# First attention: transposes by 64 rows into two banks, one PSUM rotation of four two-bank tiles, two projections to a tile

## The chip, the core and the metric

One core of a Trainium2 chip runs the whole program in one launch. The time is device microseconds from one execution. Before the change it is 716.13 us, the median of three runs (715.78 to 716.39).

The engines are TensorE (PE, with its weight loads shown apart as PEld), VectorE (DVE), ScalarE (ACT), GpSimd (POOL) and SyncE (SP, which issues most DMAs). PSUM, the memory TensorE writes its products to, has eight banks of 512 fp32 values per partition.

## The reference, cut to what matters

Two layers, each x = x + attention(norm(x)) * silu(ffn(norm(x))), for four batches of 512 tokens of width 128. The change touches only the attention of the first layer, which walks through each batch in 8 segments of 64 tokens and carries a memory M and its sum Z along (16 heads of 64):

```
q, k, v = x @ Wq, x @ Wk, x @ Wv            # per batch (8, 64, 16*64)
for each segment:                            # lax.scan
    scores  = q k^T / 8, causal
    att_dot = softmax(scores) v
    sq, sk  = elu(q) + 1, elu(k) + 1
    att_mem = sq M / (sq Z^T)
    M, Z    = M + sk^T v, Z + sum(sk)
    out     = (gate * att_mem + (1 - gate) * att_dot) @ Wo
```

The first layer's gate (its FFN), the second layer's mixture of experts and its attention over 16 channels are left as they were, but for the PSUM tiles that a few steps of the second FFN take while the first attention still runs.

## The kernel before, in words

`run` (L2310) goes through the norm and FFN of layer one, then `attn0` (L568), then `ffn1` and `attn1` of the second layer. Nearly every instruction goes through `pin` (L332), by way of `mm1`, `act1` and `vec1` (L335 to L342), which keeps it at its place in program order on its engine. So lines 336 and 339 stand for most matmuls and ScalarE steps in the profile, and the tiles tell them apart. The order of the work around the change is the order in which the code below writes it; each engine takes its own instructions in that order, and waits where a tile that it needs is not yet written or not yet free.

`attn0` has 32 segments, numbered n (8 per batch). One segment n, in program order (L833 to L877):

- `elu_exp(n+1, 0)`: ScalarE, exp and relu of q (tiles elu, up);
- `scores(n+1)`: TensorE, 16 matmuls into tile sc; VectorE evicts it (E);
- `memory(n)`: TensorE into mm; VectorE takes the reciprocal and evicts it, GpSimd applies the gate (L736);
- `elu(n+1, 0)`: VectorE (L684);
- `attended(n-2)`: four transposes of 128 rows by 128 columns into tile pa (L785); ScalarE evicts it by four instructions into attT;
- `keys(n+1)`: four such transposes into tile pk (L691); ScalarE evicts it into sk;
- `update(n)`: TensorE into mu, VectorE adds it to the memory mz (L751);
- `attend(n)`: TensorE into dot; VectorE divides, GpSimd gates and adds (L774, L775);
- `elu_exp(n+2, 1)` on ScalarE;
- up to four projection chunks of a later half batch (L601 to L642), with `scores_exp(n+1)` (ScalarE, E) behind the first of them. A chunk fills one bank: pp for q and k, with 8 matmuls that the profile shows as 16, [...]evicted by ScalarE into pj; or pv for v, evicted into vt by ScalarE (by VectorE for the first two halves), from where SP sends it to DRAM (vd) and back as vone;
- every fourth segment has no chunks but `output`: 32 matmuls (64 shown) into po.

Twelve chunks belong to each half batch: four v chunks in segments with n % 4 = 3, then four of k, then four of q. The first half's twelve chunks and two of the second's stand ahead of the loop. Steps of the second FFN (sums, normed, turned, hidden, logits, chosen, placed, up) are put in between segments 18 to 30 by a table in `run` (L2341 to L2350).

PSUM has two rotations, in one pool that stays open through `ffn1`. Tag "w" has three tiles of two banks: sc, mm, mu, dot, po (L596). Tag "t" has two tiles of one bank: pa, pk and the projection chunks (L599). The second FFN's steps use the same two tags (L924, L1006, L1038, L1072, L1081). A tile of a rotation is written again only when its last reader is done.

Of the kernel before, what the change touches and what calls it, by code (L numbers as in the profile page):

```python
# [12 lines left out]
F32 = mybir.dt.float32  # L13
# [3 lines left out]
AF = mybir.ActivationFunctionType  # L17
# [91 lines left out]
class Kernel:  # L109
# [234 lines left out]
    def pool1(self, ins):  # L344
        return self.pin(ins)

    def dma1(self, out, in_):
        return self.pin(self.nc.sync.dma_start(out=out, in_=in_))

# [215 lines left out]

    def attn0(self, xnT, g0, stack, psum, between):  # L568

# [16 lines left out]
        for k in range(4):  # L588
            t = pool.tile([P, 4, 2, DK + 1], F32, name=f"vone{k}", bufs=1)
            nc.gpsimd.memset(t[:, :, :, DK : DK + 1], 1.0)  # L590
            vone.append(t)
        qkv, vd, attT, seg = {}, {}, {}, {}

        def wide(name):

            return psum.tile([P, 2, S], F32, name=name, tag="w", bufs=3)  # L596

        def narrow(name):
            return psum.tile([P, S], F32, name=name, tag="t", bufs=2)  # L599

        def project(h):  # L601


            if h >= 2 * B:
                return []
            qkv[h] = dst = [
                pool.tile([P, 32, 64], F32, name=f"pj{h}_{wi}", tag=f"pj{wi}")
                for wi in range(2)
            ]
            vd[h] = drams.tile([2, P * 16, DK], F32, name=f"vd{h}", tag="vd")  # L610
            def chunk_v(p, k):
                ps = narrow(f"pv{h}_{p}_{k}")
                self.mm1(
                    ps, lhsT=xnT[h // 2][:, h % 2 * 2 + p, :],
                    rhs=self.wqkv[2][:, k * S : (k + 1) * S], start=True, stop=True,
                )
                t = pool.tile([P, S], F32, name=f"vt{h}_{p}_{k}", tag="vt")
                if h > 1:
                    self.act1(t, ps, AF.Copy)
                else:  # L620
                    self.vec1(nc.vector.tensor_copy(t, ps))
                nc.sync.dma_start(
                    out=vd[h][p].rearrange("(q k c) d -> k q (c d)", k=2, c=8)[k], in_=t
                )

            def chunk(wi, cq):
                ps = narrow(f"pp{h}_{wi}_{cq}").rearrange("p (c k) -> p c k", c=4)
                for c4 in range(4):
                    c = cq * 4 + c4
                    for p in range(2):  # L630
                        self.mm1(
                            ps[halves[p], c4, :],
                            lhsT=self.wqkv[wi][:, c * 64 : c * 64 + 64],
                            rhs=xnT[h // 2][:, h % 2 * 2 + p, :], start=True, stop=True,
                        )
                view = dst[wi].rearrange("d k (t c) -> d (k t) c", c=16)
                self.act1(
                    view[:, :, cq * 4 : cq * 4 + 4], ps.rearrange("d c k -> d k c"), AF.Copy
                )
            qk = [(lambda wi=wi, cq=cq: chunk(wi, cq)) for wi in (1, 0) for cq in range(4)]  # L640
            v = [(lambda p=p, k=k: chunk_v(p, k)) for p in range(2) for k in range(2)]
            return v + qk if h else qk[:4] + v + qk[4:]  # L642
# [41 lines left out]
            self.vec1(nc.vector.scalar_tensor_tensor(t, t, 1.0, up, ALU.min, ALU.add))  # L684
            seg[n][w] = t

        def turn(n, src, name):

            ps = narrow(f"{name}{n}").rearrange("p (hp c) -> p hp c", hp=4)
            for hp in range(4):  # L690
                self.pin(nc.tensor.transpose(  # L691
                    ps[:, hp], src[:, 2 * hp : 2 * hp + 2, :].rearrange("d a j -> d (a j)"),
                    self.ident,
                ))
            return ps.rearrange("p hp (x d) -> p hp x d", x=2)

        def keys(n):
            t = pool.tile([P, 4, 2, DK], F32, name=f"sk{n}", tag="sk")
            self.act1(t, turn(n, seg[n][1], "pk"), AF.Copy)
            seg[n]["sk"] = t  # L700

        def values(n):

# [71 lines left out]
            nc.gpsimd.tensor_add(t, t, seg[n]["t1"])  # L775
            seg[n]["att"] = t

        def attended(n):

            if n % 4 == 0:  # L780

                attT[n // 4] = pool.tile([P, 16, 4, 32], F32, name=f"attT{n}", tag="attT")
            ps = narrow(f"pa{n}").rearrange("p (hp c) -> p hp c", hp=4)
            for hp in range(4):
                self.pin(nc.tensor.transpose(  # L785
                    ps[:, hp, :], seg[n]["att"][:, hp].rearrange("i p v -> i (p v)"),
                    self.ident,
                ))
            src = ps.rearrange("p (a u) (h t c) -> p c a u h t", a=2, h=2, c=16)
            dst = attT[n // 4][:, :, n % 4].rearrange("p c (u y t) -> p c u y t", u=2, y=4)  # L790
            for h in range(2):
                for a in range(2):
                    self.act1(dst[:, :, :, (a + h) % 2 * 2 + a], src[:, :, a, :, h], AF.Copy)
# [20 lines left out]
        for i, chunk in enumerate(todo):  # L814
            chunk()
            if i == 4:
                elu_exp(0, 1)
            if i == 7:
                elu(0, 1)
            if i == 9:  # L820
                keys(0)
        ahead = project(1)
        for n in range(2):
            values(n)
# [8 lines left out]
        for n in range(nseg):  # L833
            if n % 4 == 3:
                todo = project((n + 1) // 4 + 1)
            elif n == 0:
                todo = ahead
            each = 2 if n == 0 else 4 if n < 3 or n % 4 != 2 else 0
            nxt = n + 1 < nseg
            more = nxt and not last(n + 1)  # L840
            if n + 2 < nseg:
                values(n + 2)
            if nxt:
                elu_exp(n + 1, 0)
                scores(n + 1)
            memory(n)
            if nxt:
                elu(n + 1, 0)
            if n > 1:
                attended(n - 2)  # L850
            if more:
                keys(n + 1)
            if not last(n):
                update(n)
            for f, *args in between.get(n - 0.5, []):
                f(*args)
            attend(n)
            ahead = n + 2 < nseg and not last(n + 2)
            if ahead:
                elu_exp(n + 2, 1)  # L860
            chunks, todo = todo[:each], todo[each:]
            for chunk in chunks[:1]:
                chunk()
            if nxt:
                scores_exp(n + 1)
            if ahead:
                elu(n + 2, 1)
            for chunk in chunks[1:]:
                chunk()
            for f, *args in between.get(n - 0.25, []):  # L870
                f(*args)
            if n % 4 == 2 and n > 4:
                output(n // 4 - 1)
            if not nxt:
                attended(n - 1)
            for f, *args in between.get(n, []):
                f(*args)  # L877
        return [lambda: attended(nseg - 1), lambda: output(2 * B - 1)]

    def begin_ffn1(self, pool, psum, layer, rooms=False):
# [37 lines left out]
        def name(what, *at):  # L920
            return "_".join(map(str, (what, layer) + at))

        def narrow(what, *at):
            return psum.tile([P, 4, P], F32, name=name(what, *at), tag="t", bufs=2)  # L924

        def sums(b):
            self.norm_sums(pool, mv, layer, range(b * 4, b * 4 + 4))
# [75 lines left out]
            self.vec1(v.tensor_add(gw[:, tiles(b), :], at[:, :, 0], at[:, :, 1]))  # L1003

        def up(b, e):
            ps = psum.tile([P, 2, S], F32, name=name("ph", b, e), tag="w", bufs=3)  # L1006
            for c in range(2):
                self.mm1(
                    ps[:, c], lhsT=self.w_in[:, e, c * P : (c + 1) * P], rhs=xnT[b],
# [24 lines left out]
        def placed(b):  # L1034


            at, idf, mask, _ = picked[b]
            ps = psum.tile([P, 4, NE], F32, name=name("pn", b), tag="t", bufs=2)  # L1038
            self.mm1(ps, lhsT=before, rhs=mask, start=True, stop=True)
            t = place[b] = pool.tile([P, 4, NE], F32, name=name("place", b), tag="place", bufs=2)  # L1040
            self.vec1(v.scalar_tensor_tensor(t, ps, 1.0, mask, ALU.add, ALU.mult))
# [23 lines left out]
        def send(b, k):  # L1065

            if k == 0:
# [1 line left out]
                    "p e (k s) -> p e k s", k=4  # L1069
                )  # L1070
                rows[b] = self.rooms.tile([NE * 4 * ROOM, D], F32, name=name("rows", b))
            ps = psum.tile([P, NE, ROOM], F32, name=name("px", b, k), tag="w", bufs=3)  # L1072
            for part in range(3):
                self.mm1(
                    ps, lhsT=parts[b][:, part, k], rhs=marks[b, k],
# [2 lines left out]
            self.act1(sent[b][:, :, k], ps, AF.Copy)  # L1078

        def up2(b, i):  # L1080
            ps = psum.tile([P, 2, 2, 4 * ROOM], F32, name=name("ph", b, i), tag="w", bufs=3)  # L1081
            for e in range(2):
                for c in range(2):
                    self.mm1(
# [1225 lines left out]
    def run(self):  # L2310
# [15 lines left out]
        with tc.tile_pool(name="wf1", bufs=1) as wf1, tc.tile_pool(name="f1", bufs=1) as f1:  # L2326
# [4 lines left out]
                xnT, g0 = self.norm_ffn0(0, lambda pool, psum: self.mixing1(pool, late, psum))  # L2331
                self.load_memory(w0)
            self.load_experts(wf1)
            with tc.tile_pool(name="ap", bufs=1, space=PSUM) as psum:
                third = ExitStack()
                self.rooms = ctx.enter_context(
                    tc.tile_pool(name="rooms", bufs=1, space=bass.MemoryType.DRAM)
                )
                first = self.begin_ffn1(f1, psum, 1, True)

                left = self.attn0(xnT, g0, stack, psum, {  # L2341
                    18: [(first.sums, 0)], 19: [(first.sums, 1)],
                    20: [(first.roots, 0, 2)], 20.5: [(first.scale, 0, 2, False), (first.normed, 0)],
                    21: [(first.turned, 0), (first.normed, 1)],
# [3 lines left out]
                    24: [(first.placed, 1)], 25: [(first.chosen, 0)],  # L2348
                    30.5: [(first.up, 0, 0)],
                })  # L2350
                second, prep = ExitStack(), []

                def begin():
# [125 lines left out]
```

## Time and profile before

| what | us |
|---|---|
| median of three runs | 716.13 |
| the profiled execution, in all | 716.71 |
| its span, from first to last instruction | 715.3 |
| busy in the span: PE | 676.8 (95%) |
| busy: DVE, ACT, POOL | 501.3, 491.1, 344.4 |
| first attention, from its first projection to the last segment | about 77 to 319 |
| projections ahead of the loop | 77 to 91.5 |
| segments 0 to 2 | 91.5 to 114 |
| segments 3 to 20 (no step of the second layer's TensorE work among them) | 114 to 241 |
| segments 21 to 26, with steps of the second FFN | 241 to 297.2 |
| segments 27 to 31, no projections left | from 297.2 |

A group line of the profile names line, engine, operation, tiles written and read, count and busy time; idle time before an instruction is put down to what ended it, the releaser. In the timeline neighbouring instructions of one group are merged: start, length from the first start to the last end, count. TensorE's instructions overlap one another, so a matmul that reads 0.27 us may be followed by the next 0.05 us later; cadence is taken from starts. The granted TensorE clock is 0.994 on average.

### The profile page before, as it was taken

To read this page: it belongs to the slowest core of one execution; us is meant where nothing else is said; L and a number is where in the kernel's file an instruction comes from. 1 tells how busy PE (TensorE), PEld (TensorE's weight loads), DVE (VectorE), ACT (ScalarE), POOL (GpSimd) and SP (SyncE) were. 2 spreads that over 40 slices of the span, in tenths; PEclk is the share of its full clock that TensorE was granted. 3 is DMA by queue.
4 is the path that set the end of the run, shared out by engine and by line. 5 is a ranking of instruction groups with operands and counts; after the bars stand their busy time and mean duration, and the time that the engine had idled before them with its cause. 6 is when DMAs were issued, how large, how long until landed. Compare 5 with 4: busy or idle time off the path is not lost.

```text
span 715.3 us, 23273 instructions
## 1 busy us (share of the span) xinstructions
PE 676.8 (95%) x9891; PEld 417.3 (58%) x9891; DVE 501.3 (70%) x1078; ACT 491.1 (69%) x809; POOL 344.4 (48%) x381
## 2 busy tenths in 40 slices
PE   7999899999999899989999999999999999999994
PEld 3666567977878768867777783332335343422433
DVE  6866376675667766875459224879896999588854
ACT  3433478786877886753553468989987999899830
POOL 7670046667576583783753333411483853312250
PEclk9999999999999998999999999999999999999999
DMA  6740243232232321200034249968949494956200
GB/s 162 159 136 0 73 131 97 48 97 71 73 97 47 91 62 48 46 4 1 1 107 146 74 148 231 244 166 176 241 146 222 121 246 130 218 144 142 60 17 19
DMA packets 84847, 79.42 MB, mean 111 GB/s; under 512 B 42512, under 2 KB 73520, under 8 KB 81664
## 3 DMA queue, kind: packets, MB, share of 16 engines
q1 hardware_dynamic: 81904, 75.12, 40.2%
q0 software_dynamic: 2256, 2.47, 1.8%
q8 instruction: 80, 1.31, 0.8%
q10 hardware_dynamic: 576, 0.26, 0.1%
q14 instruction: 31, 0.25, 0.1%
HBM read 51.62 MB, written 26.21 MB: 109 GB/s over the span
## 4 chain that ended last, share of the span: by engine, by line
PE 70%; DVE 10%; ACT 10%; issue 4%; DMA 3%; SPq 1%; POOL 1%; DVEq 0%; ACTq 0%; POOLq 0%
PE acc L336 9%; PE pp L336 8%; PE eo L336 7%; ACT e L339 7%; PE po L336 5%; PE ph L336 4%; PE pl L336 3%; PE s L336 3%; PE b L336 3%; PE pv L336 2%; PE pa L785 2%; PE pu L336 2%; PE sc L336 2%; PE pg L336 2%; PE dot L336 2%
## 5 line engine op out<-in xcount | busy, mean ns | idle before, releaser
L339 ACT ACTIVATE e<-s 128x1024 f32<-128x1024 f32 x124 | 121.9, 1054 | 13.8 <-PE s L336 13.1
L336 PE MATMUL acc<-e,strip 128*32 128x512 f32 x1000 | 124.8, 598 | 0.9 <-DVE e L1879 0.9
L339 ACT ACTIVATE e<-e 128x1024 f32<-128x1024 f32 x104 | 107.3, 1093 | 0.0
L736 POOL TENSOR_TENSOR t<-t,gate 128x512 f32<-128x512 f32 x32 | 49.8, 1555 | 63.6 <-DVE t L717 63.6
L336 PEld LDWEIGHTS acc<-e,strip 128*32 128x32 f32 x1000 | 28.7, 109 | 70.1 <-issue 58.0
L774 POOL TENSOR_TENSOR t<-t,gate 128x512 f32<-128x512 f32 x32 | 50.7, 1585 | 31.0 <-DVE sums L773 24.7
L339 ACT ACTIVATE pj<-pp 128x512 f32<-128x512 f32 x64 | 38.5, 602 | 21.1 <-PE pp L336 21.1
L684 DVE SCALAR_TENSOR_TENSOR elu<-elu,up 128x512 f32<-128x512 f32 x60 | 47.8, 797 | 4.4 <-ACT up L339 4.3
L661 DVE TENSOR_TENSOR E<-sc,cap 128x512 f32<-128x512 f32 x32 | 22.0, 688 | 35.7 <-PE sc L336 35.7
L339 ACT ACTIVATE h<-ph 128x1024 f32<-128x1024 f32 x20 | 20.5, 1024 | 37.6 <-PE ph L336 32.6
L339 ACT ACTIVATE attT<-pa 128x128 f32<-128x128 f32 x128 | 25.0, 284 | 28.5 <-PE pa L785 28.1
L336 PE MATMUL s<-q,k 64*128 64x512 bf16 x256 | 40.9, 382 | 3.5 <-ACT e L339 3.3
L336 PEld LDWEIGHTS <-k 64*128 64x128 bf16 x256 | 8.8, 94 | 59.6 <-issue 57.7
L775 POOL TENSOR_TENSOR t<-t,t 128x512 f32<-128x512 f32 x32 | 41.9, 1310 | 2.5
L336 PE MATMUL eo<-w_out,h 128*128 128x128 f32 x320 | 39.6, 278 | 0.0
L336 PEld LDWEIGHTS eo<-w_out,h 128*128 128x128 f32 x320 | 37.6, 192 | 3.4 <-issue 1.9
L1719 POOL TENSOR_TENSOR pr<-pr,pr 128x512 f32<-128x512 f32 x14 | 22.5, 1630 | 33.5 <-DVE pr L1714 33.4
L339 ACT ACTIVATE elu<-pj 128x512 f32<-128x512 f32 x60 | 38.6, 643 | 0.1
L339 ACT ACTIVATE up<-pj 128x512 f32<-128x512 f32 x60 | 38.4, 639 | 0.0
L336 PE MATMUL pp<-xnT,l0Wq 128*64 128x128 f32 x512 | 31.2, 277 | 3.2 <-ACT attT L339 2.2
L1628 DVE TENSOR_TENSOR second<-second,first 128x1024 f32<-128x1024 f32 x16 | 27.0, 1694 | 9.1 <-DMA second<-qf 9.1
L336 PE MATMUL pp<-xnT,l0Wk 128*64 128x128 f32 x512 | 32.0, 277 | 0.9 <-ACT g L339 0.7
(331 smaller groups left out, 1607.3 us busy)
## 6 DMA issues: line engine op xcount, KB each, us to landing
vd<-vt SPq DMA_DIRECT2D x32, 256.0 KB
vone<-vd SPq DMA_DIRECT2D x64, 128.0 KB
first<-qe SPq DMA_DIRECT2D x8, 1024.0 KB
second<-qf SPq DMA_DIRECT2D x16, 512.0 KB
third<-qf SPq DMA_DIRECT2D x32, 256.0 KB
qf<-qT SPq DMA_DIRECT2D x64, 64.0 KB
k<-kd SPq DMA_DIRECT2D x16, 256.0 KB
q<-qd SPq DMA_DIRECT2D x16, 256.0 KB
```

The lines of the kernel that those rows point to most:

```text
L336: return self.pin(self.nc.tensor.matmul(*args, **kw))
L339: return self.pin(self.nc.scalar.activation(*args, **kw))
L661: self.vec1(nc.vector.tensor_tensor(e, ps[:, :, 0:256].rearrange("p x (hp c) -> p x hp c", hp=4), bc(bc(self.cap, 1, 4), 1, 2), ALU.min,))
L684: self.vec1(nc.vector.scalar_tensor_tensor(t, t, 1.0, up, ALU.min, ALU.add))
L736: nc.gpsimd.tensor_mul(t, t, self.gate)
L774: nc.gpsimd.tensor_mul(t, t, gate2)
L775: nc.gpsimd.tensor_add(t, t, seg[n]["t1"])
L785: self.pin(nc.tensor.transpose(ps[:, hp, :], seg[n]["att"][:, hp].rearrange("i p v -> i (p v)"), self.ident,))
L1628: self.vec1(self.nc.vector.tensor_mul(t, t, self.first1[mm][:, two]))
L1719: self.nc.gpsimd.tensor_add(self.prod1[b, m], self.prod1[b, m], t)
```

## The change

Three things change, all for the time in which `attn0` runs.

1. **PSUM.** The pool of `attn0` is its own ("ap0"), and all its tiles come from one rotation of four tiles of two banks (`wide`, with `self.four` set). After `attn0` that pool is closed and a new one ("ap") opened with the old layout (three tiles of two banks, two of one). The last transposes and the last output come after that, from the new pool.
2. **Projections.** `half` hands out the two banks of one such tile to two chunks in turn.
3. **Transposes.** `turned(att, own)` replaces `turn`, `keys` and half of `attended`: the transposes of segment n-2's attention and of segment n+1's keys share one tile. Each old transpose of 128 rows becomes two of 64 rows (128 by 64 outputs), by the upper and the lower half of the array's rows, into the two banks. The four evictions into attT and the one into sk read across both banks.

Steps of the second FFN that used a one-bank tile take the first bank of a two-bank tile while `attn0` runs.

```diff
+    def wide(self, name):
+        bufs = 4 if self.four else 3
+        return self.banks.tile([P, 2, S], F32, name=name, tag="w", bufs=bufs)
+
+    def narrow(self, name):
+        if self.four:
+            return self.wide(name)[:, 0]
+        return self.banks.tile([P, S], F32, name=name, tag="t", bufs=2)
...
-        def wide(name):
-            return psum.tile([P, 2, S], F32, name=name, tag="w", bufs=3)
-        def narrow(name):
-            return psum.tile([P, S], F32, name=name, tag="t", bufs=2)
+        wide = self.wide
+        def half(name):
+            if not other:
+                other.append(wide(name))
+                return other[0][:, 0]
+            return other.pop()[:, 1]
...
             def chunk_v(p, k):
-                ps = narrow(f"pv{h}_{p}_{k}")
+                ps = half(f"pv{h}_{p}_{k}")
...
             def chunk(wi, cq):
-                ps = narrow(f"pp{h}_{wi}_{cq}").rearrange("p (c k) -> p c k", c=4)
+                ps = half(f"pp{h}_{wi}_{cq}").rearrange("p (c k) -> p c k", c=4)
...
-        def turn(n, src, name):
-            ps = narrow(f"{name}{n}").rearrange("p (hp c) -> p hp c", hp=4)
-            for hp in range(4):
-                self.pin(nc.tensor.transpose(
-                    ps[:, hp], src[:, 2 * hp : 2 * hp + 2, :].rearrange("d a j -> d (a j)"),
-                    self.ident,
-                ))
-            return ps.rearrange("p hp (x d) -> p hp x d", x=2)
-
-        def keys(n):
-            t = pool.tile([P, 4, 2, DK], F32, name=f"sk{n}", tag="sk")
-            self.act1(t, turn(n, seg[n][1], "pk"), AF.Copy)
-            seg[n]["sk"] = t
+        def turned(att=None, own=None):
+            ps = wide(f"tn{att}_{own}").rearrange("p x (w hp c) -> p x w hp c", w=2, hp=4)
+            each = [(0, hp, x) for hp in range(4) for x in range(2) if att is not None]
+            each += [(1, hp, x) for hp in range(4) for x in range(2) if own is not None]
+            for w, hp, x in each:
+                if w:
+                    src = seg[own][1][halves[x], 2 * hp : 2 * hp + 2, :].rearrange("d a j -> d (a j)")
+                else:
+                    src = seg[att]["att"][halves[x], hp].rearrange("i p v -> i (p v)")
+                self.pin(nc.tensor.transpose(ps[:, x, w, hp], src, self.ident[halves[x], halves[x]]))
+            if att is not None:
+                attended(att, ps[:, :, 0])
+            if own is not None:
+                t = seg[own]["sk"] = pool.tile([P, 4, 2, DK], F32, name=f"sk{own}", tag="sk")
+                self.act1(t, ps[:, :, 1].rearrange("p x hp d -> p hp x d"), AF.Copy)
...
-            if n > 1:
-                attended(n - 2)
-            if more:
-                keys(n + 1)
+            if n > 1 or more:
+                turned(n - 2 if n > 1 else None, n + 1 if more else None)
...
-            with tc.tile_pool(name="ap", bufs=1, space=PSUM) as psum:
...
+            self.four = True
+            with tc.tile_pool(name="ap0", bufs=1, space=PSUM) as self.banks:
+                left = self.attn0(xnT, g0, stack, {
...
+            self.four = False
+            with tc.tile_pool(name="ap", bufs=1, space=PSUM) as psum:
+                self.banks = psum
```

In the built program (it was built, not run) each engine's instructions stand in the same order as before, but for the transposes and one store of vt on SP. Its waits differ. In each of the 48 pairs of projection chunks, the first matmul of the second chunk waits for the eviction of the first chunk of the same tile; before, a chunk waited for the eviction of the chunk two places ahead. The four evictions into attT wait for the last transpose of the shared tile, those of the keys among them; before, for the last of pa.

## Prediction

> **What bounds the kernel now.** I read the page first (busy shares), then the busy time by stretch over the first attention, then the chain of waits through it, then the timeline of one segment. The page's head says that TensorE is nearly always busy, and that the change's stage, 77 to 319 us, is a third of the span.
>
> ```profile
> span 715.3 us, 23273 instructions
> PE 676.8 (95%) x9891; PEld 417.3 (58%) x9891; DVE 501.3 (70%) x1078; ACT 491.1 (69%) x809; POOL 344.4 (48%) x381
> ```
>
> The stretch of segments 3 to 20 says more:
>
> ```profile
> 114.00:241.00 127.00, 126.55 (x3244) 102.20 (x3246) 85.45 (x196) 96.42 (x229) 81.33 (x57) 1.00 0.29 82
> ```
>
> The columns are length, busy PE, PEld, DVE, ACT and POOL, granted clock, DMA share. TensorE is busy for 126.55 of 127 us, ScalarE for 76%. A wait given to TensorE here lengthens the stage by its whole length, and work taken from it shortens it. The chain of waits through one segment agrees:
>
> ```profile
> 212.63 0.62 PE sc L336 x32
> 213.25 0.47 PE mm L336 x32
> 213.72 0.59 PE pa L785 x4
> 214.30 0.44 PE pk L691 x4
> 214.74 0.63 PE mu L336 x32
> 215.37 0.47 PE dot L336 x32
> 215.83 3.82 PE pp L336 x64
> ```
>
> No other engine is in it. The transposes are 1.03 us of 7.03, the four projection chunks 3.82. The timeline shows how these chunks and their evictions mesh:
>
> ```profile
> 215.76 3.89 PE L336 MATMUL pp<-xnT,l0Wq 128*64 128x128 f32 x64
> ...
> 216.90 0.60 ACT L339 ACTIVATE pj<-pp 128x512 f32<-128x512 f32 x1 [0.26 <-PE pp L336]
> ...
> 217.40 0.62 ACT L339 ACTIVATE E<-E 128x512 f32<-128x512 f32 x1
> 217.92 0.59 ACT L339 ACTIVATE pj<-pp 128x512 f32<-128x512 f32 x1
> 218.56 0.85 PEld L336 LDWEIGHTS pp<-xnT,l0Wq 128*64 128x64 f32 x16 [0.15 <-ACT pj L339]
> 218.69 0.60 ACT L339 ACTIVATE pj<-pp 128x512 f32<-128x512 f32 x1 [0.19 <-PE pp L336]
> ```
>
> The first eviction starts 1.14 us after its chunk (216.90 - 215.76), takes 0.60, and TensorE goes on 0.05 after an eviction ends (217.92 + 0.59 = 218.51, load at 218.56). So a bank is free again 1.79 us after its chunk began. With two banks in turn that hides: two chunks are begun in those 1.79 us, each 0.87 (the 54.6 ns cadence of 16 matmuls, from 3.5 us for 64 without stalls).
>
> **The projections.** A chunk before waits for the eviction two chunks back; in the built program the second chunk of a tile waits for the eviction of the first. Nothing of TensorE's stands between them, since order is fixed, so the turnaround is bare. Behind the waiting matmul are queued the rest of the chunks and then sc, mm and the transposes. The second pair is not held: it needs tn evicted, long done.
> - q and k, per segment: first to second chunk 1.79, to the third 0.87, to the fourth 1.79, to sc 1.02 (as from 218.56 to 219.58): 5.47. Before: 3.82 here, 4.04 in the segment ahead (208.51 to 212.55), mean 3.93. Loss 1.54. Nine such segments in 114 to 241: +13.9.
> - v: the first eviction starts 1.20 after its chunk (201.21, 202.41) and takes 0.63. 1.88 + 0.92 + 1.88 + 1.06 = 5.74 against 3.94 (201.21 to 205.15). The third eviction also waits for the store of vt, 2.75 after the first began (202.41 to 205.16); the chunk now comes so late (2.80 + 1.20 = 4.00 after the first against 1.20 + 2.75 = 3.95) that this hides. Loss 1.80, five segments: +9.0.
>
> SP's stores of vt are issued up to 2 us later; their loads back as vone belong to segments at least two later, 14 us, so nothing waits. In no-projection segments the four-tile rotation asks only for readers that are done in the trace by then.
>
> **The transposes.** Eight of 128 by 128 now have a cadence of 0.109 us (0.33 busy for one, 0.66 for four): 0.87. The change makes 16 of them, with 64 moving columns, in two row halves. Nearest row: po, which runs 64 by 128 tiles in two row halves into two banks, 64 matmuls in 3.77 us of the chain, 0.118 per pair with 128 columns. So halves do run side by side. With 64 columns a pair needs 0.055 for the matmul, and its two loads: the loads of pa are 0.06 apart (two cover 0.20 us, one takes 0.14). I take 0.06 per pair: 8 pairs, 0.48, saving 0.39 with both parts, 0.20 with one.
>
> A rule speaks against it. The Trainium skill, "TensorE: Matmul & The Clock Gate", section "LDWEIGHTS (loading the stationary operand)", says a load's time goes by its columns and not by its rows: 32 by 128 costs what 128 by 128 does, columns / 1.2, which is 0.107 us here. The change doubles the loads and leaves each at 128 columns. By the rule, 8 pairs are 0.86 and the gain is nil, and 1.7 us if loads of the two halves don't overlap. The trace's 0.06 for a load in a transpose is about half the rule's figure, and po shows overlap, so I take the row. By the rule the sum below would be 7 to 11 us higher. Bounds for a full set: -0.43 (0.055 a pair, the moving columns alone) to +0.40 (16 loads that overlap in part).
>
> In 114 to 241 there are 18 sets with attention (x72 of pa) and 16 with keys (x64 of pk): 16 x 0.39 + 2 x 0.20 = -6.6.
>
> attT's eviction waits now for the keys' transposes too: it starts about 0.1 after mu begins, where it started 0.33 ahead of it. ScalarE then does attT 0.64, sk 0.48, elu and up 0.52 each, and comes to the first projection eviction 1.18 after the chunk's start, instead of 1.14. Nearly covered; I leave 0.04 out.
>
> **The sum.**
> - 77 to 91.5: six full pairs before the first scores, 0.87 each, 5.2, less 1.0 of stalls that are there now (0.92 at the change from v to q): +4.2.
> - 91.5 to 114: five pairs, 4.4, less transposes 0.8, and 0.4 for waits on VectorE that are there anyway (1.19 ahead of pk at 100.46): +3.2.
> - 114 to 241: 13.9 + 9.0 - 6.6 = +16.3.
> - 241 to 297.2: TensorE has 5.8 us idle here (50.36 of 56.2 busy). In segment 21 the chunks already wait 2.3 us for attT's eviction, so only the last pair counts (+0.8); 23 has idle time between v and the logits, whose tile is now free at once (-1.5); 24 and 25 +1.1 and +1.5; 22 and 26 wait for VectorE, -0.1: +1.8.
> - 297.2 to 319: no chunks, VectorE is 19.49 of 21.8 busy and on the path: -0.3 at most.
> - the new pool: the second expert matmul (ph at 322.17) waits for attT's last evictions, which ScalarE does behind h: about 323.25. +1.1.
>
> Together +26.3. 716.7 + 26.3 = 743.0 for a profiled execution, which lies 0.6 above the median of the runs: 742.4, say 742.
>
> **The rivals.**
> 1. *The 64-row transposes gain nothing* (loads at the rule's price, or no overlap). About 28 sets: +11: 753. For it: twice the loads of the same width. Against: po.
> 2. *The clock falls.* Two gaps of 0.9 us in each 8.3 could lower the granted clock; from 271.8 on, mm takes 0.78 us instead of 0.43, after about 4 us of idleness. Against: gaps of 1.2 us at 99 and 1.4 at 305 left the clock whole. A tenth of the stage at half clock costs 15 to 20: about 760.
> 3. *Faster: the wait is cheap.* If ScalarE turned a half around much faster, TensorE would keep the transposes' gain (some 9 us in all) and lose the stalls it has now on pj and vt (3.9 and 8.4 by the weight loads, mostly overlapped, perhaps 3): 716 - 12 = 704. The point where signs turn: about 0.2 us of bare wait for each of 48 pairs, against 0.92 (1.79 - 0.87) in the trace. Only a wait that isn't felt could do this, as where TensorE already waits for something later.
>
> Slower as reckoned, 735 to 749: 0.74; rival 1: 0.14; rival 2: 0.06; rival 3, and less than reckoned: 0.06. The range, 735 to 757, leaves 2 in 10 out. A measurement of this kernel tells 0.2% (1.4 us) from no change: faster 0.03, same 0.02, slower 0.95.
>
> **What would show it.** In the new timeline, in every full segment: some 0.7 us of idle PE in each pair of pp (0.92 less what the last matmul's own length covers), ended by ACT pj (vt for v); sc to sc 8.2 to 8.6 us, where it was 7.0 to 7.4; idle PE of 114 to 241 up from 0.5 to some 20 us. tn: 16 transposes in about 0.5 us, pairs 0.06 apart; 0.9 or more speaks for rival 1. The granted clock in that stretch at 1.00; less is rival 2. Wrong altogether if the second chunk starts before its tile's first eviction has ended.

## The result, and the profile after

| | before | after |
|---|---|---|
| median of the runs, us | 715.95 (713.23 to 716.39, 4 runs) | 747.14 (743.64 to 752.38, 4 runs) |
| the profiled execution, in all | 716.71 | 752.38 |
| its span | 715.3 | 750.7 |
| segments 3 to 20 | 127.3 | 146.7 |

The changed kernel is slower: 1.045 times the time before, with a 95% interval of 1.0383 to 1.0517. Its profiled execution is the slowest of its four runs, 5.2 above their median. The page's head:

```profile
span 750.7 us, 23770 instructions
PE 674.3 (90%) x10131; PEld 411.2 (55%) x10131; DVE 497.7 (66%) x1078; ACT 492.8 (66%) x809; POOL 346.2 (46%) x381
```

TensorE is busy 2.5 us less than before (676.8) in a span 35.4 us longer. It has 240 instructions more, the halved transposes, but not more work: it waits. Segments 3 to 20 now run from 123.16 to 269.89. First their busy time (columns as before), then the waits of TensorE there: who waited, for whom, us in all, times, longest.

```profile
123.16:269.89 146.73, 123.62 (x3385) 98.34 (x3385) 82.99 (x196) 98.22 (x229) 84.52 (x58) 1.00 0.25 71
```

```profile
PE pp L336 <- ACT pj L339: 12.8, 18, 0.8
PE pv L336 <- ACT vt L339: 8.3, 10, 1.2
```

TensorE is idle for 23.1 us (146.73 - 123.62), where the stretch before had 0.5. 21.1 of them are ended by an eviction of a projection, 28 times: two pairs in each of the 14 segments with projections. The granted clock of the stretch is 1.00. The chain of waits through segment 9, its chunks of q among them:

```profile
173.16 0.66 PE tn L709 x16
...
173.84 0.79 ACT attT L339 x4
174.63 0.49 ACT sk L339
175.12 0.51 ACT elu L339
175.62 0.52 ACT up L339
176.14 0.50 ACT pj L339
...
176.68 1.99 PE pp L336 x32
...
178.69 0.61 ACT pj L339
...
179.34 1.09 PE pp L336 x16
```

Before, this chain held TensorE alone. Now it crosses to ScalarE and back twice in a segment. In the first pair it does not even run through the chunk's own matmuls: ScalarE comes to that chunk's eviction only when attT, sk, elu and up are done. The timeline of the same chunks:

```profile
174.82 1.09 PE L336 MATMUL pp<-xnT,l0Wq 128*64 128x128 f32 x16
...
176.00 0.63 ACT L339 ACTIVATE pj<-pp 128x512 f32<-128x512 f32 x1
...
176.68 1.97 PE L336 MATMUL pp<-xnT,l0Wq 128*64 128x128 f32 x32 [0.77 <-ACT pj L339]
...
178.69 0.60 ACT L339 ACTIVATE pj<-pp 128x512 f32<-128x512 f32 x1 [0.28 <-PE pp L336]
...
179.34 1.09 PE L336 MATMUL pp<-xnT,l0Wq 128*64 128x128 f32 x16 [0.70 <-ACT pj L339]
```

The chunk begun at 174.82 is evicted from 176.00 to 176.63, and only then, at 176.68, does its neighbour in the same tile begin: 1.86 us behind it. The third chunk follows the second at once (177.60), being in another tile. The fourth comes 1.74 behind the third. The data do not ask for this wait: the eviction reads one bank, and the next chunk writes the other. It stands in the built program, which counts the two banks as one tile.

### The profile page after: what moved, and what is told of

It reads as the page before. It is cut to its first block, busy times and chain, and to the rows that moved or that the text cites. A ratio compares the mean times of both kernels' runs of the same rounds, so it can differ in the third digit from the quotient of the medians.

```text
span 750.7 us, 23770 instructions
## 1 busy us (share of the span) xinstructions
PE 674.3 (90%) x10131; PEld 411.2 (55%) x10131; DVE 497.7 (66%) x1078; ACT 492.8 (66%) x809; POOL 346.2 (46%) x381
## 4 chain that ended last, share of the span: by engine, by line
PE 66%; ACT 15%; DVE 9%; issue 5%; DMA 2%; SPq 1%; POOL 1%; DVEq 0%; ACTq 0%; POOLq 0%
PE pp L336 8%; PE acc L336 8%; PE eo L336 7%; ACT e L339 7%; PE po L336 5%; PE ph L336 4%; PE pv L336 3%; PE b L336 3%; PE pl L336 3%; ACT pj L339 3%; PE s L336 3%; PE sc L336 2%; PE pg L336 2%; PE pu L336 2%; PE tn L709 2%
## 5 line engine op out<-in xcount | busy, mean ns | idle before, releaser
L750 POOL TENSOR_TENSOR t<-t,gate 128x512 f32<-128x512 f32 x32 | 52.5, 1640 | 102.3 <-DVE t L731 102.3
L339 ACT ACTIVATE pj<-pp 128x512 f32<-128x512 f32 x64 | 38.4, 600 | 49.4 <-PE pp L336 49.4
L788 POOL TENSOR_TENSOR t<-t,gate 128x512 f32<-128x512 f32 x32 | 49.6, 1549 | 23.2 <-DVE sums L787 16.2
L336 PE MATMUL pp<-xnT,l0Wq 128*64 128x128 f32 x512 | 35.3, 287 | 13.5 <-ACT pj L339 13.2
L336 PE MATMUL pv<-l0Wv,xnT 128*128 128x512 f32 x64 | 34.1, 632 | 14.3 <-ACT vt L339 10.3
L339 ACT ACTIVATE h<-ph 128x1024 f32<-128x1024 f32 x20 | 20.5, 1024 | 39.6 <-PE ph L336 32.3
L336 PE MATMUL pp<-xnT,l0Wk 128*64 128x128 f32 x512 | 34.7, 284 | 12.9 <-ACT pj L339 11.4
L336 PEld LDWEIGHTS pp<-xnT,l0Wq 128*64 128x64 f32 x512 | 29.0, 142 | 18.8 <-ACT pj L339 17.2
L336 PEld LDWEIGHTS pp<-xnT,l0Wk 128*64 128x64 f32 x512 | 28.6, 141 | 17.8 <-ACT pj L339 15.4
L339 ACT ACTIVATE up<-pj 128x512 f32<-128x512 f32 x60 | 38.4, 639 | 0.0
```

Source lines behind the costliest of these rows:

```text
L336: return self.pin(self.nc.tensor.matmul(*args, **kw))
L339: return self.pin(self.nc.scalar.activation(*args, **kw))
L750: nc.gpsimd.tensor_mul(t, t, self.gate)
L788: nc.gpsimd.tensor_mul(t, t, gate2)
```

## The experiments

The theory (called A below): the loss is the bare turnaround of a bank pair, put between neighbouring chunks by sharing a tile; the 64-row transposes by themselves gain. The rivals: the transposes or the new rotation cost the time; sharing a tile costs by itself, whatever the order. Twelve kernels were run in three series: 1 to 4, 5 to 8 and 9 to 12, the second on another chip than the other two. Each ratio is to the kernel before in the same series, whose median was 715.65 in the first, 711.83 in the second and 716.56 in the third. The expectations were reckoned from a kernel before at some 716 us, so times of the second series are compared by their ratio. The table gives lengths from the profiled executions, from one sc to the next: segment 3 (v), 12 (k), 9 (q), 6 (output), then the length of segments 3 to 20. Segment 12 is the longest k segment before; the other four take 7.39 to 7.40.

| kernel | time, us | ratio (95%) | v | k | q | out | 3 to 20 |
|---|---|---|---|---|---|---|---|
| before | 715.95 | 1 | 7.08 | 7.68 | 7.03 | 6.54 | 127.3 |
| after | 747.14 | 1.0450 (1.0383 to 1.0517) | 8.47 | 8.75 | 8.38 | 6.35 | 146.7 |
| 1 a tile for each chunk | 712.11 | 0.9948 (0.9933 to 0.9964) | 6.46 | 8.12 | 6.47 | 6.35 | 124.3 |
| 2 before, 64-row transposes | 727.80 | 1.0193 (1.0137 to 1.0249) | 7.01 | 7.79 | 6.96 | 6.91 | 132.5 |
| 3 after, 128-row transposes | 751.58 | 1.0513 (1.0461 to 1.0565) | 8.85 | 8.75 | 8.75 | 6.55 | 151.1 |
| 4 before, shared tiles | 752.93 | 1.0518 (1.0464 to 1.0571) | 8.81 | 8.69 | 8.69 | 6.54 | 149.6 |
| 5 after, halves interleaved | 716.58 | 1.0071 (1.0047 to 1.0095) | 6.75 | 9.45 | 6.72 | 6.35 | 130.0 |
| 6 after, one eviction for a pair | 705.87 | 0.9912 (0.9889 to 0.9935) | 6.46 | 7.62 | 6.47 | 6.35 | 121.5 |
| 7 = 1, three vt | 700.08 | 0.9841 (0.9817 to 0.9866) | 6.46 | 6.47 | 6.47 | 6.66 | 118.0 |
| 8 = before, three vt | 706.47 | 0.9929 (0.9906 to 0.9952) | 7.08 | 7.05 | 7.03 | 6.54 | 125.2 |
| 9 = 6, three vt | 705.36 | 0.9852 (0.9825 to 0.9878) | 6.46 | 6.47 | 6.47 | 6.35 | 117.3 |
| 10 = after, three vt | 746.81 | 1.0443 (1.0411 to 1.0476) | 8.42 | 8.48 | 8.38 | 6.36 | 145.4 |
| 11 = 7, 128-row transposes | 707.68 | 0.9885 (0.9860 to 0.9910) | 6.84 | 6.85 | 6.85 | 6.55 | 122.8 |
| 12 = 2, three vt | 717.16 | 1.0012 (0.9995 to 1.0029) | 7.01 | 6.96 | 6.96 | 6.91 | 126.4 |

### 1. A tile for each chunk

```diff
-        def half(name):
-            if not other:
-                other.append(wide(name))
-                return other[0][:, 0]
-            return other.pop()[:, 1]
+        half = self.narrow
```

> The changed kernel, but every projection chunk takes a two-bank tile of the same rotation for itself and uses its first bank; 64-row transposes and the rotation of four stay. Theory A (the loss is the second chunk's wait for the eviction of the first in its tile): the wait is gone, the transposes' gain stays; 700 to 708 us, sc to sc about 6.5 us in full segments, idle PE in the chunks near nothing. Rival B (one rotation of four is too tight for all tiles): nine tiles per segment instead of seven make it worse, 745 us or more. Rival C (the 64-row transposes or the new pool cost time too): 716 to 725.

The loss is gone, and a little more: 35 us below the changed kernel, all else of the change kept. So sharing with an eviction in between makes the loss. But 712.1 is not the 700 to 708 that was expected. The q and v segments are as short as reckoned, the k segments behind v are not. The timeline of this kernel's segment 4 shows why:

```profile
118.95 0.60 ACT L339 ACTIVATE vt<-pv 128x512 f32<-128x512 f32 x1 [1.13 <-DMA vd<-vt]
...
120.95 0.60 ACT L339 ACTIVATE vt<-pv 128x512 f32<-128x512 f32 x1 [1.40 <-DMA vd<-vt]
...
121.60 0.70 PE L336 MATMUL dot<-vone,E 64*64 64x65 f32 x32 [0.53 <-ACT vt L339]
...
123.80 2.84 PE L336 MATMUL pp<-xnT,l0Wk 128*64 128x128 f32 x48 [0.47 <-ACT sk L339]
```

vt, the tile in which a v chunk waits for its store to DRAM, has two buffers. The third and fourth v evictions wait for the stores of the first two to DRAM, and ScalarE stands with everything queued behind. In the built program dot takes the tile of the fourth v chunk and waits for its eviction (dot begins 1.23 us behind mu, where 0.52 is usual), and the second k chunk takes the tile of tn and waits for sk, which ScalarE reaches late (1.57 behind the first chunk, instead of 0.91). Together 1.4 us. Experiments 7 to 12 follow this up.

### 2. The old layout with the 64-row transposes

The kernel before, with `turned` in place of `turn`, `keys` and the transposes of `attended`, its tile taken from the old rotation of three.

```diff
-            if n > 1:
-                attended(n - 2)
-            if more:
-                keys(n + 1)
+            if n > 1 or more:
+                turned(n - 2 if n > 1 else None, n + 1 if more else None)
```

> The kernel before with the 64-row transposes alone: the shared transpose tile comes from the rotation of three two-bank tiles, chunks keep their two one-bank tiles. Theory A: about 0.38 us less in each of some 28 sets, less about 0.15 where dot now waits for mm's eviction in a rotation of three: 706 to 711 us. Rival C: 716 or more.

A miss, and the transposes are not what failed: they take the same 0.06 us a pair. Most of what they save is lost at the next wait. Five tiles of a segment go through a rotation of three, and dot takes the tile of mm, so it can start only when mm is evicted: in segment 9 of experiment 12, the same layout, mu began 1.74 us after sc (156.50 - 154.76) instead of 2.12 (149.22 - 147.10 in experiment 8's segment 8), yet dot 2.51 instead of 2.63. The two lines of it:

```profile
156.43 0.69 DVE L719 TENSOR_TENSOR t<-mm,rm 128x512 f32<-128x512 f32 x1
...
157.24 0.59 PEld L336 LDWEIGHTS dot<-vone,E 64*64 64x64 f32 x32 [0.19 <-PE mu L336]
```

The view names mu as the releaser; VectorE's eviction of mm ends at 157.12, and dot's first load follows 0.12 later. That dot waits for it is read from the tile and these times, and no run tests it alone. Output segments are 0.37 longer for it. One more thing is dear, and it is again vt. This kernel's segment 4 lasted 11.14 instead of 7.39:

```profile
124.33 0.60 ACT L339 ACTIVATE vt<-pv 128x512 f32<-128x512 f32 x1 [2.67 <-DMA vd<-vt]
...
128.01 0.64 ACT L339 ACTIVATE pj<-pp 128x512 f32<-128x512 f32 x1
...
128.70 3.59 PE L336 MATMUL pp<-xnT,l0Wk 128*64 128x128 f32 x32 [2.29 <-ACT pj L339]
```

A store held ScalarE for 2.67 us; elu, up, attT and sk were queued behind; the first projection of this segment was evicted late, and TensorE stood 2.29 us and then ran two chunks at half speed (3.59 instead of 1.97): its granted clock was 0.50 from 128.84 to 132.25. This execution took 723.30, the least of the four, so the trace shows 6.6 us of the loss (over the 716.71 of the profiled execution before) and not all 12 of the median.

### 3. The changed kernel with transposes of 128 rows

Eight transposes of 128 by 128 into the shared tile, attention in its first bank, keys in the second.

```diff
-            for w, hp, x in each:
...
-                self.pin(nc.tensor.transpose(ps[:, x, w, hp], src, self.ident[halves[x], halves[x]]))
+            for w, n in enumerate((att, own)):
+                for hp in range(4) if n is not None else ():
...
+                    self.pin(nc.tensor.transpose(ps[:, w, hp], src, self.ident))
```

> The changed kernel with eight transposes of 128 rows in the shared tile (attention in the first bank, keys in the second) in place of sixteen of 64 rows; sharing and rotation stay. Theory A: the transposes are on the path, 0.38 us per full set, 28 sets: 10 to 12 us above the changed kernel, 756 to 760. Rival C: as the changed kernel or faster, 747 or less.

The direction is A's, the size is not. The q and v segments are 0.37 and 0.38 longer, as reckoned; the k segments 4, 12 and 20 are not longer at all (8.75 against 8.85, 8.75 and 9.02). Segments 3 to 20 come to 151.1 against 146.7: the transposes of 64 rows gain 4.4 us there. On the whole time the two intervals overlap.

### 4. The kernel before with shared tiles

`half` as in the change, its tiles from the old rotation of three; transposes as before.

```diff
-                ps = narrow(f"pp{h}_{wi}_{cq}").rearrange("p (c k) -> p c k", c=4)
+                ps = half(f"pp{h}_{wi}_{cq}").rearrange("p (c k) -> p c k", c=4)
```

> The kernel before with the sharing alone: two chunks to a two-bank tile out of the old rotation of three, transposes of 128 rows in one-bank tiles. Theory A: the loss without the transposes' gain, 716 + 42 = 758 us (752 to 762), PE idle ahead of the second chunk of each pair, ended by its tile's first eviction. Rival B: no rotation of four here, so 716 to 722.

A holds: sharing alone makes all of the loss, 1.0518, and a little more. The waits of TensorE in its segments 3 to 20 are those of the changed kernel:

```profile
PE pp L336 <- ACT pj L339: 12.5, 18, 0.7
PE pv L336 <- ACT vt L339: 7.8, 10, 1.3
```

### 5. Two open tiles, halves in the order A, B, A, B

```diff
-        def half(name):
-            if not other:
+        def half(name, ahead=2):
+            if not closing:
                 other.append(wide(name))
-                return other[0][:, 0]
-            return other.pop()[:, 1]
+                if len(other) == ahead:
+                    closing.append(True)
+                return other[-1][:, 0]
+            ps = other.pop(0)
+            if not other:
+                closing.clear()
+            return ps[:, 1]
```

> The changed kernel with its tiles still shared, two chunks to a tile, but two tiles open at once and the halves handed out in the order A first, B first, A second, B second. So the second chunk of a tile still waits for the first one's eviction, but that one was issued two chunks earlier instead of one. Theory A (the loss is that the bare turnaround of 1.79 us lies between neighbouring chunks, with 0.87 of work to cover it): the wait is covered by the chunk of the other tile, q and k segments fall from 8.4 to 6.5 us, the tile that mu takes is held by the last v chunk, so k segments stay at about 7.6 as with tiles of their own: 712 us (708 to 717). Theory B (sharing a tile costs by itself, through evictions or banks, whatever the order): 740 or more.

The same tiles, as many of them, the same evictions, two to a tile; only the order of the halves differs (the v chunks of half batch 1, ahead of the loop, keep the old one). The q segment falls from 8.38 to 6.72. So what costs is the distance between two chunks of a tile, and not sharing as such. The waits for the evictions of q and k are down to this, in segments 3 to 20,

```profile
PE pp L336 <- ACT pj L339: 1.3, 3, 0.4
```

and those of pv for its own to 0.7. The order is not free, though. By the ratio the kernel is 0.7% slower than before, which would be 721 us where 708 to 717 was expected, and 1.2% slower than experiment 1. The q segment is 0.25 longer than there. In segment 12 TensorE stands 1.27 us ahead of dot for the last v eviction, held by its store.

### 6. One eviction for a pair

The q and k chunks of a pair fill both banks; one ScalarE instruction evicts 1024 elements after the second. v chunks have tiles of their own.

```diff
+                if not cq % 2:
+                    return
                 view = dst[wi].rearrange("d k (t c) -> d (k t) c", c=16)
                 self.act1(
-                    view[:, :, cq * 4 : cq * 4 + 4], ps.rearrange("d c k -> d k c"), AF.Copy
+                    view[:, :, cq * 4 - 4 : cq * 4 + 4], ps.rearrange("d c k -> d k c"), AF.Copy
                 )
```

> The changed kernel with the q and k chunks still two to a tile, but nothing read from the tile between them: one ScalarE instruction of 1024 elements evicts both chunks after the second. The v chunks have a tile each. Theory A: no wait is left between the chunks of a pair; q segments 6.5 us, and ScalarE loses one fixed cost per pair: 710 us (706 to 715). Theory B (two chunks in one tile of two banks slow each other, on TensorE's or ScalarE's side): the q and k segments stay at 8 or more, 730 to 745. A middle way: the eviction comes so late (2.0 us after the pair began, 1.1 long) that mu, which takes the tile of the second pair four tiles later, waits for it; then about 0.5 us more in each of 24 segments, 722.

As A has it: with no reader between the two chunks of a tile, the tile can be shared for nothing, and the q segment takes 6.47. The eviction of 1024 takes 1036 ns at the mean (32 of them) where two of 512 took 2 x 600, so ScalarE does 6 us less (32.5 against 38.4).

### 7 and 8. A third buffer for vt, in the new layout and in the old

```diff
-                t = pool.tile([P, S], F32, name=f"vt{h}_{p}_{k}", tag="vt")
+                t = pool.tile([P, S], F32, name=f"vt{h}_{p}_{k}", tag="vt", bufs=3)
```

> The changed kernel with a tile for each chunk, and with three instead of two buffers for vt, so that the third v eviction of a half batch no longer waits for the first store to DRAM. With two buffers the k segments behind v lasted 7.6 to 8.1 us where q segments lasted 6.47: sc stood 0.76 and dot 0.67 us for v evictions that waited for a store. If that is why so little was gained (712.1 instead of 700 to 708), these five to seven segments lose 1 to 1.5 us each: 705 us (702 to 709). If the k segments are longer for another reason: 712.

> The kernel before, with three instead of two buffers for vt and nothing else: it tells whether the third buffer helps the layout with four tiles in turn only, or the old one too. In the old layout a v chunk waits on its own bank, k segments last 7.39 where q segments last 7.03, so at most 0.4 us in each of 7 half batches, some 2 us: 713.5 us (711 to 716). If it gains as much as with own tiles of the new layout (6 us or more, 710 or less), the store was the larger limit of both.

With a tile for each chunk (the expectation's 0.76 for sc is a wait of the weight load alone, beside matmuls that ran on to 118.71, and was no loss; dot's was) the third buffer brings another 1.1% (0.9948 to 0.9841), and the k segments fall to 6.47 (but for segment 8, 7.35, with a gap of 0.56 in its first chunk for which the view names no wait). The group of v evictions on ScalarE, of experiment 1 and then of 7 (after the bar: busy time, mean ns, idle time before and what ended it):

```profile
L339 ACT ACTIVATE vt<-pv 128x512 f32<-128x512 f32 x24 | 14.7, 612 | 14.7 <-DMA vd<-vt 9.5 <-PE sc L336 2.2 <-PE mu L336 1.5
```

```profile
L339 ACT ACTIVATE vt<-pv 128x512 f32<-128x512 f32 x24 | 14.3, 617 | 4.4 <-DMA vd<-vt 2.1 <-PE sc L336 1.3 <-PE pv L336 0.8
```

In the old layout it brings 0.7% (706.47), more than the 2 us expected: 2.1 us are in segments 3 to 20 (127.3 to 125.2), and segment 23 alone is 2.2 shorter (11.49 to 9.29). Some 1.2 of that is the clock, an estimate: it was 0.50 in the last 2.4 us of this segment before (from 269.44), and whole in it here. The store was a limit of both layouts. What the change without its sharing is worth beside it is 7 against 8: 0.9841 to 0.9929, some 6 us.

### 9 to 12. What is left of each part when the store is out of the way

9 is experiment 6 with the third buffer, 10 the changed kernel, 11 experiment 7 with 128-row transposes (the edit of 3), 12 experiment 2.

> One eviction for each pair of q and k chunks, a tile for each v chunk, and three buffers for vt: two projections to a tile as in the changed kernel, with no eviction between them and no wait for the store. If the k segments behind v (7.6 with two buffers, 6.47 with three where each chunk has its tile) lose the same here, 5 to 7 us come off 705.9: 699.5 us (697 to 702), level with a tile for each chunk (700.1). If the eviction of 1024 comes too late for mu's tile, the k and q segments show it once the store is gone: 704 or more.

Level with 7 (intervals 0.9825 to 0.9878 and 0.9817 to 0.9866), in a series in which the kernel before itself was 4.7 us slower: two projections to a tile cost nothing when evicted together.

> The changed kernel with a third buffer for vt and nothing else. My theory: with shared tiles the third v eviction comes so late, behind the wait for the first eviction, that the store hides; only the k segments behind v (8.85 where q has 8.35) lose up to 0.45 us in some of 7 half batches: 745 us (742 to 748), as against 747.1. If the store was part of the loss of sharing, it falls by 6 us or more, to 741 or less.

As expected, no more than 0.1% of the time: the store isn't part of the loss. With shared tiles the third v chunk comes so late that its buffer is free; in the changed kernel ScalarE waited for the store 0.4 us in all, where it had waited 9.6 before:

```profile
L339 ACT ACTIVATE vt<-pv 128x512 f32<-128x512 f32 x24 | 14.5, 603 | 14.3 <-PE pv L336 13.9 <-DMA vd<-vt 0.4
```

> A tile for each chunk and three buffers for vt, but the old eight transposes of 128 rows in the shared tile of attention and keys. It prices the 64-row transposes where nothing else stops TensorE: 0.38 us in each full set, 0.2 in each half set. Of 28 sets with attention some 22 lie where TensorE sets the time: 16 x 0.38 + 6 x 0.2 = 7.3 more than with 64 rows (700.1): 707 us (705 to 710). If the transposes gain nothing where all else flows, 700 to 702.

Where nothing else stops TensorE, 64 rows gain 0.38 in a full segment (6.85 to 6.47; not in 8 and 19), and 4.9 us in segments 3 to 20. On the whole, 0.9885 against 0.9841 is 0.0044, give or take 0.0035 by the two intervals: 3 us, 1 to 6, instead of 7.

> The kernel before with the 64-row transposes in its rotation of three (the second kernel tried), and three buffers for vt. There the time rose to 727.8, by one stall of 4 us behind a v eviction that waited for its store, with elu, attT and sk queued behind it on ScalarE, and by gaps of the second FFN's stretch; dot's wait for mm's eviction took back the 0.4 that the transposes had saved. If the store is what made it slow, the third buffer brings it to the old layout with three buffers (706.5) plus little for output segments that are 0.4 longer: 709 us (705 to 714). If the rotation of three with five tiles to a segment is the cause: 718 or more.

Between the two expectations, nearer to the second. The third buffer takes away the stall of 4 us (segment 4 lasts 7.02), and the ratio falls from 1.0193 to 1.0012; but the same transposes in the rotation of three remain 0.8% slower than experiment 8. In segments 3 to 20 it is 1.1 us longer, the output segments 0.37 each; the larger part lies behind, in segments 21 to 28 (64.3 us against 60.1 by the traces). Most of these 4.2 us are the clock: it was at 0.50 for 10.24 us here (267.97 to 278.21) and for 3.41 in experiment 8 (266.59 to 270.00), so that 5.1 and 1.7 us of work were lost, an estimate from half the lengths. What brought the clock down longer was not settled.

## Why the prediction was right, point by point

742 was forecast, 747.14 came: 31.2 us more than before, where 26.3 was reckoned. The likeliest case was the right one, and its mechanism is shown by 1, 4, 5 and 6. For the profiled execution, 5.2 us above the median, the trace shows 35.4, the span's growth. Where the 9.1 us between that and the 26.3 lie:

| stretch | reckoned | measured |
|---|---|---|
| up to the first projection | 0 | +1.3 |
| projections ahead of the loop | +4.2 | +4.4 |
| segments 0 to 2 | +3.2 | +3.5 |
| segments 3 to 20 | +16.3 | +19.4 |
| segments 21 to 26 | +1.8 | +4.2 |
| what follows | +0.8 | +2.6 |

**The projections.** Reckoned +13.9 and +9.0, 22.9 for segments 3 to 20; sharing alone (4) added 22.2 (149.6 - 127.3). The turnaround was put at 1.79 and is 1.86 and 1.74: the first eviction starts 1.18 behind its chunk, the length that the prediction reckoned and left out, and the second 1.09. A v segment was to lose 1.80 and lost 1.73 (8.81 - 7.08), a q segment 1.54 and lost 1.66. That the store hides behind the late third chunk was right (10).

A rule of the Trainium skill ("Perfetto Trace Analysis", section "Matmuls") would have independent matmul groups rotate through different PSUM banks, so that the eviction of one overlaps the next one's matmuls. The changed kernel does this to the letter, neighbouring chunks are in different banks, and they didn't overlap: the wait goes by the tile, and two banks of one tile are one to it. With the banks of two tiles in turn (5) they did, but for the 0.25 us above.

**The transposes.** Sixteen were reckoned at 0.48 us; in segment 9 the first load starts at 173.083 and the last matmul at 173.574, the pairs of loads are 0.06 apart, and the two loads of a pair mostly 2 to 4 ns. So the rule of the Trainium skill ("TensorE: Matmul & The Clock Gate", section "LDWEIGHTS (loading the stationary operand)"), that a load costs its columns over 1.2, 0.107 us here, does not hold for these loads: 16 of them in 8 x 0.107 would have been 0.86, and rival 1 falls with it. The term that was off is "16 x 0.39 + 2 x 0.20 = -6.6": the gain is 4.4 by experiment 3. It counted every set as on the path; in three of the k segments TensorE lost the gain at once in other gaps (dot broke off for 0.31 in segment 4; the profile names no cause), and output segments 10 and 18, and v segment 19, gained nothing.

**The layout.** The prediction let the rotation of four cost nothing. Experiment 3 is experiment 4 in the new layout, with one tile for both kinds of transposes, and is 1.5 us longer in segments 3 to 20. So the 19.4 measured part into 22.2 + 1.5 - 4.4. These are differences of neighbouring kernels' lengths, which must add up; what makes the 1.5 was not traced.

**Segments 21 to 26.** Segment 21 was to lose 0.8 and lost 3.1 (9.90 to 13.03). This is rival 2 in small. The busy time of stretches of it (columns as above; the granted clock is the third figure from the end):

```profile
273.80:276.30 2.50, 0.01 (x1) 0.00 (x0) 1.57 (x4) 2.50 (x9) 0.00 (x0) 1.00 0.45 103
...
277.30:278.90 1.60, 1.60 (x20) 1.57 (x16) 1.53 (x6) 0.60 (x1) 0.46 (x1) 0.50 0.05 10
...
284.00:286.00 2.00, 2.00 (x80) 1.72 (x72) 1.78 (x4) 1.44 (x6) 0.20 (x1) 1.00 0.00 0
```

The second chunk already waits for the first one's eviction, which is behind a table load on ScalarE; TensorE stands 2.55 us, starts again at 276.35, and from 277.3 to 284 has half its clock. The same stretch before stood 2.2 us and kept its clock. Over segments 21 to 26 the clock was at 0.50 for 6.83 us before (269.44 to 276.27) and for 10.24 after (277.19 to 284.02 and 307.91 to 311.32). Half of each is lost work, an estimate: 3.4 us before and 5.1 after. This difference of 1.7 is the larger part of the 2.4 missed.

**What follows.** ph waits 0.95 us for attT's last evictions (reckoned 1.1). The other 1.6 us were not traced.

**Up to the first projection.** The change alters nothing there, and the +1.3 is the clock of this one execution. The busy time of that stretch, after and then before:

```profile
14.36:17.77 3.41, 3.41 (x10) 1.65 (x9) 1.06 (x4) 0.75 (x2) 0.81 (x2) 0.50 1.00 257
```

```profile
14.00:18.00 4.00, 3.82 (x22) 2.36 (x22) 2.54 (x7) 1.19 (x2) 1.42 (x3) 1.00 1.05 249
```

The matmul of pg ahead of it starts at 13.85 (before at 13.79), that of pw behind it at 18.52 (before at 17.23): the whole 1.3. TensorE had stood 2.91 us ahead of pg, and 2.25 before. The trace of experiment 10 has no half clock there, and that of experiment 5 has one from 14.22. With the 1.7 above, some 3.0 of the 9.1 us are the clock.

**The rivals.** Rival 3 had it that "only a wait that isn't felt" could turn the sign, from 0.2 us for each of 48 pairs. The waits are felt in full, 0.75 us each in segments 3 to 20 (21.1 / 28). Rival 2 had the clock fall under the gaps of each segment; in segments 3 to 20 it stayed at 1.00, and it fell only where TensorE stood longer. Its price of 15 to 20 us was too high for a tenth of the stage's time: half of a tenth of some 268 us (319 - 77 + 26) is 13. Experiments 6 and 9 show the forecast of rival 3 nearly come true in another way: take the reader from between the chunks, and the rest of the change is a gain.

## What to carry to other kernels

A tile that is filled in parts is best read once, when it is full, or filled in turn with another one: a reader between two writers of one tile puts its whole turnaround (eviction's start, length and release, 1.74 to 1.86 us here) between them, and the work that stands between the writers (0.87 us, the first chunk itself) is all that covers it. Count the distance in the engine's order from a buffer's last reader to its next writer before counting buffers: the change gave the projections more PSUM and took away the one chunk that had hidden their evictions. When such a wait is gone, look for what it had covered: the buffers of vt, one stage further down, held back more than the better layout had gained without them (0.9948, and 0.9841 with a third).

## What the runs showed of the hardware

- Transposes in two row halves of the array run side by side: 16 of 64 rows in 0.49 us (segment 9 of the changed kernel) against 8 of 128 rows in 0.87 (before).
- A pause of 2.55 us of TensorE was followed, 0.8 us after its end, by 6.8 us at a clock of 0.50; one of 1.93 us (305.18 to 307.11), also 0.8 after its end, by 3.4 us; one of 2.29 us in experiment 2, 0.14 after its end, by 3.4 us. In the kernel before, a pause of 1.31 us (267.11 to 268.42) was followed by 6.8 us, and one of 2.2 us by none, so the length of the pause alone does not tell it. In all these traces a stretch at 0.50 that ended before the kernel did lasted 3.41, 6.83 or 10.24 us. The Trainium skill ("TensorE: Matmul & The Clock Gate", section "HAM oscillation — how this bites in real kernels") warns of gaps above about 3.4 us; here shorter ones were followed by the half clock; that they brought it about is not shown.
- A ScalarE eviction of 512 elements took 0.60 us and one of 1024 took 1.04 (experiment 6), so some 0.16 us of each do not grow with the elements (2 x 0.60 - 1.04, an estimate).
